# The last five groups of a gather-and-sum pass: what goes ahead of a group's sums, and in which order the sums go

## Chip, core and metric

The kernel runs on one core of a Trainium2 chip. The metric is the device time of one execution in microseconds. Five engines work beside each other and meet through semaphores: PE (TensorE, matrix products), DVE (VectorE), ACT (ScalarE), POOL (GpSimd) and SP (SyncE). DMAs are issued from SP, ACT and POOL. Each engine carries out its instructions in the order in which the program lists them.

## The reference, cut

One layer of a graph network over 12,500 nodes with 256 features and 200,000 edges (float32 throughout). The edges are sorted by destination.

```python
h = jnp.maximum(_layernorm(x, axis=-1), 0.0)
agg = jax.ops.segment_sum(h[src], dst, num_segments=N)
z = (1.0 + eps_gin) * h + agg
t = jnp.dot(z, W1) + b1                      # 256 -> 512
t = jax.nn.relu(_batchnorm(t, g1, bt1))      # over all nodes
conv_out = jnp.dot(t, W2) + b2               # 512 -> 256
out = jax.nn.relu(_batchnorm(conv_out + h, g2, bt2))
return x + out
```

The two batch norms need the mean and variance over all nodes, so the second product can't start before the first is complete for every node, and the output not before the second is.

## The kernel before

Three passes follow each other. The first makes t for all nodes and its statistics, the second makes conv_out + h and its statistics, the third the output. The change lies in the first.

Nodes are cut into NCH = 25 chunks of 512 (the last, chunk 24, has 212), edges into 1563 tiles of 128. GT = 12 tiles are a group, so there are NG = 131 groups, numbered 0 to 130; the last has three tiles. Since the edges are sorted, group i reaches nodes in a window of 256 from 96 i - 64 on; a program part not shown here takes over if they don't. For the end of the pass this gives: chunk 22 is last reached by group 123, chunk 23 by groups up to 128, chunk 24 by groups 127 to 130.

What is done for a group i, with the name of the helper:

- gather(i), L435: one indirect DMA on POOL per tile fetches 128 rows of h. The tiles of a group are fetched from the last to the first, each into its own slot of the group's buffer (gt, or gta and gtb together). There are five buffers, and gathers run AHEAD = 4 groups ahead.
- edges(i), L464: DVE builds the 0/1 matrices oh that say which edge goes to which of 128 node offsets.
- sums(i), L478: PE adds up, in one PSUM tile ps, twelve products of a slot's oh and its rows. The loop over j goes from slot 0 up, and slot 0 is the one fetched last.
- hold(i), L485: ACT copies ps to zs. spots(i), L489: DVE builds a matrix at that says where the 128 offsets lie in the window. put(i), L496: two products place zs in the window (pz).
- add(i), L507: DVE adds pz to the one or two chunks (zc) that the window reaches. z_load and z_scale fetch a chunk of transposed h and multiply it by 1 + eps.

Once the last group of a chunk has been added, its four slices follow: slice_of(c, f), L514, two products with W1 into ph (two PSUM buffers); take(c, f), L525 to L528, statistics on DVE, a copy to ts on ACT and a store of ts to t_tab issued by ACT.

All of the first pass is scheduled by hand: the loop at L550 writes the instructions out, and every engine keeps that order. A step i of this loop does, in this order: gather(i + 4), the adds up to group i - 4, take of the slice of the step before, spots and hold of group i - 2, edges(i + 1), sums(i), put(i - 2), and one slice from the queue of ready chunks. After the last group four more steps (131 to 134) bring the late groups in, with adds up to i - 3 and all queued slices.

Two lines that set this order:

```python
                    while added <= min(i - late, NG - 1):   # late: 4 for i < NG, else 3
                        add(added)
...
                    while whole < NCH and last(whole) < (before if i < NG else added):
                        queue += [(whole, f) for f in range(HC)]
```

After the loop, norm (L272 to L284) turns the statistics into scale and offset. The second pass (L623 on) loads a chunk of t (ti, three buffers, the first three loaded well before) and of transposed h (yT) on SP's queue, applies the activation on ACT (L630) and runs eight products per chunk into py (L637).

Of the kernel before, what the change touches and what calls it, by code (L numbers as in the profile page):

```python
# [19 lines left out]
AHEAD = 4  # L20
LEAD = 30
# [6 lines left out]
COPIES = 2  # L28
GROUP = 4
GAHEAD = 3  # L30


@with_exitstack
def kernel(
# [21 lines left out]
    HC = H // P  # L56
    CH = P * R
    NCH = -(-N // CH)
# [3 lines left out]
    for g in range(NCH):  # L62
        rows = min(CH, N - g * CH)
# [7 lines left out]
    full_tiles = E // P  # L71
    left = E - full_tiles * P
    NG = -(-NTILE // GT)
    STEP = -(-N * P * GT // E)
    WIDE = P + 2 * MARGIN
    NBLK = -(-max(NTILE, NG * GT) // P)
# [43 lines left out]
    def slot(ga, t):  # L120

        if len(ga) == 1:
            return ga[0][:, t, :]
        return ga[0][:, t, :] if t < LOW else ga[1][:, t - LOW, :]
# [26 lines left out]
    with ExitStack() as es:  # L151
# [5 lines left out]
        whole = E // PART  # L157
# [9 lines left out]
        with tc.issue_after(placed.ins):  # L167
# [30 lines left out]
        first = raw.tile([P, P], F32, name="first")  # L198
# [4 lines left out]
            pb, lhsT=first, rhs=dstT[:, : NG * GT].rearrange("p (g t) -> p g t", t=GT)[:, :, 0],  # L203
            start=True, stop=True,
# [42 lines left out]
        some = raw.tile([1, 1], F32, name="some")  # L247
# [59 lines left out]
    def fast():  # L307

        parts = []
        for n0, w in chunks:  # L310
            n = w * R
# [20 lines left out]
        with ExitStack() as fs:  # L332
# [8 lines left out]
            with ExitStack() as es:  # L341
# [87 lines left out]
                def gather(i):  # L429
                    t0, n = groups[i]  # L430
                    k = i % (AHEAD + 1)
                    ga = lands[k] if k < EARLY else (gat.tile([P, GT, D], F32, name="gt"),)
                    for t in reversed(range(t0, t0 + n)):
                        rows = left if t == full_tiles else P
                        nc.gpsimd.indirect_dma_start(  # L435
                            out=slot(ga, t - t0)[:rows], out_offset=None, in_=x if i < LEAD else h_tab,
                            in_offset=bass.IndirectOffsetOnAxis(ap=srcT[:rows, t : t + 1], axis=0),
                        )
                    gathered[i] = ga
# [16 lines left out]
                def z_scale(c):  # L456
                    n = chunks[c][1] * R
                    nc.scalar.activation(zc[c][:, :, :n], zc[c][:, :, :n], AF.Copy, scale=gin1)

                def edges(i):  # L460

                    t0, n = groups[i]
                    ohs[i] = sel.tile([P, GT, P], F32, name="oh", bufs=3)
                    nc.vector.tensor_tensor(  # L464
                        ohs[i][:, :n, :],
                        col[:, :P].unsqueeze(1).to_broadcast([P, n, P]),
                        dstT[:, t0 : t0 + n].unsqueeze(2).to_broadcast([P, n, P]),
                        op=OP.is_equal,
                    )

                def sums(i):

                    t0, n = groups[i]
                    ga, oh = gathered.pop(i), ohs.pop(i)
                    ps = ps_s.tile([P, D], F32, name="ps")
                    for j in range(n):
                        rows = left if t0 + j == full_tiles else P
                        nc.tensor.matmul(  # L478
                            ps, lhsT=oh[:rows, j, :], rhs=slot(ga, j)[:rows], start=(j == 0), stop=(j == n - 1)
                        )  # L480
                    summed[i] = ps

                def hold(i):
                    zss[i] = sel.tile([P, D], F32, name="zs", bufs=3)
                    nc.scalar.copy(zss[i], summed.pop(i))  # L485

                def spots(i):
                    ats[i] = sel.tile([P, WIDE], F32, name="at", bufs=3)
                    nc.vector.tensor_scalar(ats[i], col, shift[:, i : i + 1], None, op0=OP.is_equal)  # L489

                def put(i):

                    zs, at = zss.pop(i), ats.pop(i)
                    pz = ps_z.tile([P, DC, WIDE], F32, name="pz2")
                    for d in range(DC):
                        nc.tensor.matmul(  # L496
                            pz[:, d, :], lhsT=zs[:, d * P : (d + 1) * P], rhs=at, start=True, stop=True
                        )
                    placed[i] = pz

                def add(i):
                    lo, hi = span(i)
                    pz = placed.pop(i)
                    for c in reach(i):
                        a, b = max(lo, c * CH, 0), min(hi, (c + 1) * CH, N)
                        side = zc[c][:, :, a - c * CH : b - c * CH]
                        nc.vector.tensor_add(side, pz[:, :, a - lo : b - lo], side)  # L507

                def slice_of(c, f):

                    n = chunks[c][1] * R
                    ph = ps_t.tile([P, CH], F32, name="ph")
                    for d in range(DC):
                        nc.tensor.matmul(  # L514
                            ph[:, :n], lhsT=w1s[:, d, f * P : (f + 1) * P],
                            rhs=zc[c][:, d, :n], start=(d == 0), stop=(d == DC - 1),
                        )
                    slices[c, f] = ph
                    if f == HC - 1:
                        del zc[c]  # L520

                def take(c, f):
                    n = chunks[c][1] * R
                    ph = slices.pop((c, f))
                    nc.vector.bn_stats(st1[:, f, c, :], ph[:, :n])  # L525
                    ts = tsp.tile([P, CH], F32, name="ts")
                    nc.scalar.copy(ts[:, :n], ph[:, :n])  # L527
                    nc.scalar.dma_start(t_tab[c, :, f, :n], ts[:, :n])  # L528

                def first(c):  # L530

                    return min(i for i in range(NG) if c in reach(i))

                def last(c):
                    return max(i for i in range(NG) if c in reach(i))
# [6 lines left out]
                settle(gathered[0], GT // 2, GT, gathered[0], "g")  # L542
                queue, loads, scales, taken = [], {}, {}, []
                for c in range(NCH):
                    k = max(first(c) + 1, c + 2)
                    loads.setdefault(k, []).append(c)
                    scales.setdefault(max(first(c) + 3, c + 3), []).append(c)
                    assert c + 1 < k <= first(c) + 4 and c < LEAD - AHEAD
                added = whole = 0
                for i in range(NG + 4):  # L550
                    before = added
                    if i + AHEAD < NG:
                        gather(i + AHEAD)

                    late = 4 if i < NG else 3
                    while added <= min(i - late, NG - 1):
                        add(added)
                        added += 1
                    for c, f in taken:
                        take(c, f)  # L560
                    taken = []
                    if 0 <= i - 2 < NG:
                        spots(i - 2)
                        hold(i - 2)
                    if i + 1 < NG:
                        edges(i + 1)

                    if i < NCH:
                        h_chunk(i)
                    if i + 1 < min(LEAD, NG):  # L570
                        settle(gathered[i + 1], GT // 2, GT, gathered[i + 1], "g")
                    for c in scales.get(i, ()):
                        z_scale(c)

                    if i < NG:
                        sums(i)
                    if 0 < i <= NCH:
                        turn(i - 1)
                        turn_out(i - 1)
                    if 0 <= i - 2 < NG:  # L580
                        put(i - 2)
                    for c in loads.get(i, ()):
                        z_load(c)
                    while whole < NCH and last(whole) < (before if i < NG else added):
                        queue += [(whole, f) for f in range(HC)]
                        whole += 1
                    if i < NG:
                        some = queue[:1]
                    else:
                        some = queue  # L590
                    queue = queue[len(some):]
                    if i < NG:
                        for c, f in some:
                            slice_of(c, f)
                        taken = some
                    else:
                        for c, f in some:
                            slice_of(c, f)
                            take(c, f)
                assert added == NG and whole == NCH and not queue and not taken and not zc, (queue, taken, list(zc))  # L600

            sc1, of1 = norm(keep, st1, mv1, HC, g1c, bt1c, b1c, "1")

# [320 lines left out]
```

## Time and profile before

| | |
|---|---|
| Time, three runs | 2235.57 us median (2233.42 to 2241.05) |
| Profiled execution | 2235.88 us, span 2233.7 us |
| Granted PE clock over the span | 0.834 |
| PE busy, POOL busy | 1478.6 us, 1480.4 us |
| From the last gather to the first py | POOL's last gather starts at 1958.31, the first py at 2000.51 |
| Second pass on PE | 2000.51 to 2170.2 |
| End | 2233.7 |

How to read the rows: times are microseconds from the start of the span. A timeline row has start, duration, engine, line, operation, output and inputs, shapes and a count, and in brackets the idle time ahead of it with what ended it. Line numbers are those of the kernel before. A float32 matrix product leaves two records, so that twelve sums stand as x24. The ends of matmuls are modelled. A row of the chain has start, duration and what the time went to.

### The profile page before, as it was taken

To read this page: it belongs to the slowest core of one execution; us is meant where nothing else is said; L and a number is where in the kernel's file an instruction comes from. 1 tells how busy PE (TensorE), PEld (TensorE's weight loads), DVE (VectorE), ACT (ScalarE), POOL (GpSimd) and SP (SyncE) were. 2 spreads that over 40 slices of the span, in tenths; PEclk is the share of its full clock that TensorE was granted. 3 is DMA by queue.
4 is the path that set the end of the run, shared out by engine and by line. 5 is a ranking of instruction groups with operands and counts; after the bars stand their busy time and mean duration, and the time that the engine had idled before them with its cause. 6 is when DMAs were issued, how large, how long until landed. Compare 5 with 4: busy or idle time off the path is not lost.

```text
span 2233.7 us, 15142 instructions
## 1 busy us (share of the span) xinstructions
PE 1478.6 (66%) x4874; PEld 1066.5 (48%) x4874; DVE 716.5 (32%) x1092; ACT 510.1 (23%) x963; POOL 1480.4 (66%) x1575
## 2 busy tenths in 40 slices
PE   3567677667666666656666666666666666679994
PEld 2455545545444544544454444444444544444443
DVE  5566656531222122122212221211221121124345
ACT  4666666520000000000000000000000000034445
POOL 7777777777777777777777777777777777700000
PEclk9888888888888788878877887888887788789998
DMA  6677767644444444444444444444443444438739
GB/s 196 208 228 232 246 218 237 183 128 120 129 128 129 116 128 129 120 123 129 131 116 125 132 120 125 129 117 126 129 133 113 126 128 118 130 131 320 252 118 311
DMA packets 157615, 349.47 MB, mean 156 GB/s; under 512 B 30104, under 2 KB 82452, under 8 KB 154454
## 3 DMA queue, kind: packets, MB, share of 16 engines
q0 software_dynamic: 75008, 204.90, 32.8%
q1 hardware_dynamic: 54224, 104.03, 13.9%
q10 hardware_dynamic: 28294, 39.47, 4.9%
q8 instruction: 41, 0.67, 0.1%
q14 instruction: 48, 0.39, 0.1%
HBM read 284.28 MB, written 64.00 MB: 156 GB/s over the span
## 4 chain that ended last, share of the span: by engine, by line
POOL 52%; issue 22%; PE 11%; ACT 6%; DVE 4%; DMA 4%; ACTq 0%; SPq 0%; DVEq 0%; POOLq 0%
POOL gt L435 32%; POOL gta L435 12%; PE py L637 8%; POOL gtb L435 6%; DMA gt<-in_x_dram,srcT 3%; ACT gt L381 2%; DVE stg L370 2%; PE ps L478 2%; PE ph L514 1%; ACT yT L657 1%; ACT gta L381 1%; DMA out_dram<-xr 1%; DVE oh L464 1%; POOL gta L212 1%; ACT gtb L381 0%
## 5 line engine op out<-in xcount | busy, mean ns | idle before, releaser
L478 PE MATMUL ps<-gt,oh 128*128 128x256 f32 x1872 | 577.0, 481 | 402.5 <-DMA gt<-h_tab,srcT 321.5
L435 POOL DMA_INDIRECT gt<-h_tab,srcT x720 | 680.7, 945 | 219.3 <-issue 219.3
L478 PEld LDWEIGHTS ps<-gt,oh 128*128 128x128 f32 x1872 | 459.1, 250 | 546.0 <-issue 315.7
L478 PE MATMUL ps<-gta,oh 128*128 128x256 f32 x838 | 291.9, 524 | 270.5 <-DMA gta<-h_tab,srcT 212.1
L478 PEld LDWEIGHTS ps<-gta,oh 128*128 128x128 f32 x838 | 224.8, 275 | 352.4 <-issue 198.3
L525 DVE BATCH_NORM_STATS2 st<-ph 128x6 f32<-128x512 f32 (+1 forms) x100 | 68.4, 684 | 971.2 <-PE ph L514 971.2
L435 POOL DMA_INDIRECT gta<-h_tab,srcT x323 | 305.2, 945 | 98.4 <-issue 95.9
L527 ACT COPY ts<-ph 128x512 f32<-128x512 f32 (+1 forms) x100 | 57.4, 574 | 1326.5 <-DVE st L525 1326.5
L435 POOL DMA_INDIRECT gt<-in_x_dram,srcT x216 | 204.2, 945 | 65.8 <-issue 60.9
L464 DVE TENSOR_TENSOR oh<-col,dstT 128x1536 f32<-128x1536 f32 x131 | 227.7, 1738 | 0.0
L514 PE MATMUL ph<-zc,w1s 128*128 128x512 f32 (+1 forms) x400 | 193.1, 610 | 20.6 <-DVE hc L423 20.1
L507 DVE TENSOR_TENSOR zc<-pz,zc 128x512 f32<-128x512 f32 (+8 forms) x187 | 93.9, 520 | 282.5 <-PE pz L496 244.2
L435 POOL DMA_INDIRECT gtb<-h_tab,srcT x160 | 151.2, 945 | 48.7 <-issue 47.5
L637 PE MATMUL py<-gta,w2s 128*128 128x512 f32 (+1 forms) x400 | 169.6, 587 | 3.7 <-ACT gta L630 3.7
L496 PE MATMUL pz<-at,zs 128*128 128x256 f32 x524 | 134.9, 380 | 5.0 <-ACT zs L485 5.0
L637 PEld LDWEIGHTS py<-gta,w2s 128*128 128x128 f32 x400 | 76.4, 192 | 96.4 <-issue 75.7
L514 PEld LDWEIGHTS ph<-zc,w1s 128*128 128x128 f32 x400 | 78.3, 199 | 79.8 <-issue 49.1
L381 ACT ACTIVATE gt<-gt,nbg,rsg 128x256 f32<-128x256 f32 x216 | 108.1, 586 | 9.1 <-DVE nbg L379 8.1
L496 PEld LDWEIGHTS pz<-at,zs 128*128 128x128 f32 x524 | 97.6, 190 | 19.1 <-ACT zs L485 7.1
L630 ACT ACTIVATE gta<-ti,of,sc 128x512 f32<-128x512 f32 (+1 forms) x100 | 79.6, 803 | 82.9 <-PE py L637 78.8
L478 PE MATMUL ps<-gtb,oh 128*128 128x256 f32 x416 | 98.3, 379 | 0.0
L435 POOL DMA_INDIRECT gta<-in_x_dram,srcT x80 | 75.6, 946 | 24.4 <-issue 8.5
(97 smaller groups left out, 897.3 us busy)
## 6 DMA issues: line engine op xcount, KB each, us to landing
t_tab<-ts ACTq DMA_DIRECT2D x96, 256.0 KB
ti<-t_tab SPq DMA_DIRECT2D x24, 1024.0 KB
xt<-in_x_dram SPq DMA_DIRECT2D x24, 512.0 KB
h_tab<-ht ACTq DMA_DIRECT2D x24, 512.0 KB
h_cols<-hc SPq DMA_DIRECT2D x24, 512.0 KB
zc<-h_cols SPq DMA_DIRECT2D x24, 512.0 KB
yT<-h_cols SPq DMA_DIRECT2D x24, 512.0 KB
gt<-h_tab,srcT POOLq DMA_INDIRECT x720, 2.8
```

The lines of the kernel that those rows point to most:

```text
L370: nc.vector.bn_stats(st[:, c : c + 2, :].rearrange("p c s -> p (c s)"), two.rearrange("p c d -> p d c"),)
L381: nc.scalar.activation(slot(to, c), slot(v, c), AF.Relu, bias=nb[:, c : c + 1], scale=rs[:, c : c + 1])
L435: nc.gpsimd.indirect_dma_start(out=slot(ga, t - t0)[:rows], out_offset=None, in_=x if i < LEAD else h_tab, in_offset=bass.IndirectOffsetOn ...
L464: nc.vector.tensor_tensor(ohs[i][:, :n, :], col[:, :P].unsqueeze(1).to_broadcast([P, n, P]), dstT[:, t0 : t0 + n].unsqueeze(2).to_broadcas ...
L478: nc.tensor.matmul(ps, lhsT=oh[:rows, j, :], rhs=slot(ga, j)[:rows], start=(j == 0), stop=(j == n - 1))
L496: nc.tensor.matmul(pz[:, d, :], lhsT=zs[:, d * P : (d + 1) * P], rhs=at, start=True, stop=True)
L507: nc.vector.tensor_add(side, pz[:, :, a - lo : b - lo], side)
L514: nc.tensor.matmul(ph[:, :n], lhsT=w1s[:, d, f * P : (f + 1) * P], rhs=zc[c][:, d, :n], start=(d == 0), stop=(d == DC - 1),)
L525: nc.vector.bn_stats(st1[:, f, c, :], ph[:, :n])
L527: nc.scalar.copy(ts[:, :n], ph[:, :n])
L630: nc.scalar.activation(tT[:, f, :n], ti[:, f, :n], AF.Relu, bias=of1[:, f : f + 1], scale=sc1[:, f : f + 1],)
L637: nc.tensor.matmul(py[:, :n], lhsT=w2s[:, f, d * P : (d + 1) * P], rhs=tT[:, f, :n], start=(f == 0), stop=(f == HC - 1),)
```

## The change

A constant CLOSE = 5 cuts the loop in two. Steps 0 to 125 run as before (without the cases that only the end needed). Steps 126 to 131 have a loop of their own:

- spots(i), spots of the two groups still open, edges(i + 1) and the scaling of chunk 24 come first; chunk 24 is loaded in step 125 and scaled in step 126 (before: 128 and 130).
- Then every earlier group is finished ahead of this group's sums: hold and put of each group up to i - 1, and all adds up to i - 1.
- Then all slices of chunks that are complete by now, each with its take.
- Then sums(i), with the slots in the order in which they were fetched, from the last slot down to slot 0.

In the listing of the changed program's instructions this gives, on PE: placing of 124 and 125, four slices of chunk 22, sums of 126; placing of 126, sums of 127; placing of 127, sums of 128; placing of 128, four slices of chunk 23, sums of 129; placing of 129, sums of 130; placing of 130, four slices of chunk 24. POOL's and SP's lists are the same as before; of SP's waits, the loads of the first yT no longer stand behind late stores of ts: the first waits for a load of its own queue, the second and third for the second and third store of chunk 23.

```diff
+CLOSE = 5
...
                     ps = ps_s.tile([P, D], F32, name="ps")
-                    for j in range(n):
+                    order = list(range(n)) if i < NG - CLOSE else list(reversed(range(n)))
+                    for j in order:
                         rows = left if t0 + j == full_tiles else P
                         nc.tensor.matmul(
-                            ps, lhsT=oh[:rows, j, :], rhs=slot(ga, j)[:rows], start=(j == 0), stop=(j == n - 1)
+                            ps, lhsT=oh[:rows, j, :], rhs=slot(ga, j)[:rows], start=(j == order[0]), stop=(j == order[-1])
                         )
...
                 for c in range(NCH):
-                    k = max(first(c) + 1, c + 2)
+                    k = min(max(first(c) + 1, c + 2), NG - CLOSE - 1)
                     loads.setdefault(k, []).append(c)
-                    scales.setdefault(max(first(c) + 3, c + 3), []).append(c)
+                    scales.setdefault(min(max(first(c) + 3, c + 3), NG - CLOSE), []).append(c)
...
-                for i in range(NG + 4):
+                for i in range(NG - CLOSE):
...
+                near = NG - CLOSE - 2
+                for c, f in taken:
+                    take(c, f)
+                for i in range(near, NG - CLOSE):
+                    spots(i)
+                for i in range(NG - CLOSE, NG + 1):
+                    if i + AHEAD < NG:
+                        gather(i + AHEAD)
+                    if i < NG:
+                        spots(i)
+                    if i + 1 < NG:
+                        edges(i + 1)
+                    for c in scales.get(i, ()):
+                        z_scale(c)
+                    while near < i:
+                        hold(near)
+                        while added < near - 1:
+                            add(added)
+                            added += 1
+                        put(near)
+                        near += 1
+                    while added < near:
+                        add(added)
+                        added += 1
+                    while whole < NCH and last(whole) < added:
+                        queue += [(whole, f) for f in range(HC)]
+                        whole += 1
+                    for c, f in queue:
+                        slice_of(c, f)
+                        take(c, f)
+                    queue = []
                     if i < NG:
-                        for c, f in some:
...
+                        sums(i)
```

More of the change, by code (lines that the diff above doesn't have):

```diff
@@ L73 @@
     NG = -(-NTILE // GT)
+    assert max(LEAD, NCH) < NG - CLOSE
     STEP = -(-N * P * GT // E)
@@ L544, in fast @@
                 for c in range(NCH):
-                    k = max(first(c) + 1, c + 2)
+                    k = min(max(first(c) + 1, c + 2), NG - CLOSE - 1)
                     loads.setdefault(k, []).append(c)
-                    scales.setdefault(max(first(c) + 3, c + 3), []).append(c)
+                    scales.setdefault(min(max(first(c) + 3, c + 3), NG - CLOSE), []).append(c)
                     assert c + 1 < k <= first(c) + 4 and c < LEAD - AHEAD
                 added = whole = 0
-                for i in range(NG + 4):
+                for i in range(NG - CLOSE):
                     before = added
[L552 to L556, printed above, removed]
+                    gather(i + AHEAD)
+                    while added <= i - 4:
                         add(added)
@@ L560, in fast @@
                         take(c, f)
-                    taken = []
-                    if 0 <= i - 2 < NG:
+                    if i >= 2:
                         spots(i - 2)
                         hold(i - 2)
-                    if i + 1 < NG:
-                        edges(i + 1)
+                    edges(i + 1)
                     if i < NCH:
                         h_chunk(i)
-                    if i + 1 < min(LEAD, NG):
+                    if i + 1 < LEAD:
                         settle(gathered[i + 1], GT // 2, GT, gathered[i + 1], "g")
@@ L573, in fast @@
                         z_scale(c)
-                    if i < NG:
-                        sums(i)
+                    sums(i)
                     if 0 < i <= NCH:
@@ L579, in fast @@
                         turn_out(i - 1)
-                    if 0 <= i - 2 < NG:
+                    if i >= 2:
                         put(i - 2)
@@ L583, in fast @@
                         z_load(c)
-                    while whole < NCH and last(whole) < (before if i < NG else added):
+                    while last(whole) < before:
                         queue += [(whole, f) for f in range(HC)]
                         whole += 1
-                    if i < NG:
[L588 to L591, printed above, removed]
-                    if i < NG:
-                        for c, f in some:
[L594 to L599, printed above, removed]
@@ L600, in fast @@
-                assert added == NG and whole == NCH and not queue and not taken and not zc, (queue, taken, list(zc))
+                    taken = queue[:1]
+                    queue = queue[1:]
+                    for c, f in taken:
+                        slice_of(c, f)
+                near = NG - CLOSE - 2
+                for c, f in taken:
+                    take(c, f)
[3 more added lines that the diff above has]
+                    if i + AHEAD < NG:
+                        gather(i + AHEAD)
+                    if i < NG:
+                        spots(i)
+                    if i + 1 < NG:
+                        edges(i + 1)
+                    for c in scales.get(i, ()):
[14 more added lines that the diff above has]
+                    for c, f in queue:
+                        slice_of(c, f)
+                        take(c, f)
+                    queue = []
+                    if i < NG:
+                        sums(i)
@@ L602, in fast @@
+                assert added == near == NG and whole == NCH and not zc, list(zc)
             sc1, of1 = norm(keep, st1, mv1, HC, g1c, bt1c, b1c, "1")
```

## The prediction

> **What bounds the kernel now.** I read the page's busy times first, then the chain that ended last, then the timelines of the engines around the end of the gathers.
>
> ```profile
> PE 1478.6 (66%) x4874; PEld 1066.5 (48%) x4874; DVE 716.5 (32%) x1092; ACT 510.1 (23%) x963; POOL 1480.4 (66%) x1575
> POOL 52%; issue 22%; PE 11%; ACT 6%; DVE 4%; DMA 4%; ACTq 0%; SPq 0%; DVEq 0%; POOLq 0%
> ```
>
> PE and POOL have the same share of the span, but the chain goes through POOL and its issue gaps for 74%: the gathers set the pace. On POOL's timeline one gather starts every 1.25 us (0.95 busy, 0.30 between) without a break, up to these:
>
> ```profile
> 1954.59 0.94 POOL L435 DMA_INDIRECT gt<-h_tab,srcT  x1 [0.30 <-issue]
> ...
> 1958.31 0.95 POOL L435 DMA_INDIRECT gta<-h_tab,srcT  x1 [0.30 <-issue]
> ```
>
> These are the last gathers of groups 129 and 130 (130 has three). After them nothing is left for POOL, and the chain of waits runs over PE:
>
> ```profile
> 1954.59 4.04 DMA gt<-h_tab,srcT
> 1958.77 8.08 PE ps L478 x24
> 1967.71 1.73 PE ph L514 x4
> ...
> 1990.22 1.15 PE pz L496 x4
> 1991.78 3.21 PE ph L514 x8
> 2000.51 169.65 PE py L637 x400
> ```
>
> From the landing of group 129 at 1958.77 to the first product of the second pass (py) at 2000.51 lie 41.7 us. This is the only place where the change can bring something, and the change lies in it. PE's timeline shows what fills it (24 records are 12 matmuls, two records each):
>
> ```profile
> 1942.44 7.72 PE L478 MATMUL ps<-gt,oh 128*128 128x256 f32 x24 [5.73 <-DMA gt<-h_tab,srcT]
> 1950.86 1.88 PE L514 MATMUL ph<-zc,w1s 128*128 128x512 f32 x4
> 1958.77 8.08 PE L478 MATMUL ps<-gt,oh 128*128 128x256 f32 x24 [6.03 <-DMA gt<-h_tab,srcT]
> ...
> 1969.27 1.65 PE L478 MATMUL ps<-gta,oh 128*128 128x256 f32 x6
> 1971.61 1.13 PE L496 MATMUL pz<-at,zs 128*128 128x256 f32 x4 [0.69 <-ACT zs L485]
> 1972.58 1.88 PE L514 MATMUL ph<-zc,w1s 128*128 128x512 f32 x4
> 1976.63 1.13 PE L496 MATMUL pz<-at,zs 128*128 128x256 f32 x4 [2.18 <-ACT zs L485]
> 1977.60 10.44 PE L514 MATMUL ph<-zc,w1s 128*128 128x512 f32 x20
> 1990.22 1.13 PE L496 MATMUL pz<-at,zs 128*128 128x256 f32 x4 [2.18 <-ACT zs L485]
> 1991.78 5.02 PE L514 MATMUL ph<-zc,w1s 128*128 128x212 f32 x16 [0.42 <-DVE zc L507]
> 2000.51 9.69 PE L637 MATMUL py<-gta,w2s 128*128 128x512 f32 x18 [3.71 <-ACT gta L630]
> ```
>
> PE idles some 6 us ahead of each group, since the sums begin with the slot that lands last; then 12 sums run in one burst, 8 us behind the landing. Behind it wait placings that are two groups late and seven wide slices (one at 1967.71, one at 1972.58, five from 1977.60) that could have run earlier: chunk 22 has its last edges in group 123 and chunk 23 in group 128.
>
> **The change part by part.**
>
> *Sums in the order of landing.* No instruction is added. At full clock a sum takes 0.43 us, from the row below with 16 records of double width in 6.80 us (0.425 us each, two to a matmul, half the width), at half clock twice that. One group arrives in 12 x 1.25 = 15 us, so PE keeps up, and only the last sum is left when the last slot lands.
>
> ```profile
> 1974.40:1977.80 3.40, 1.22 (x6) 1.00 0.20 77
> 1977.80:1981.20 3.40, 3.40 (x5) 0.50 0.00 0
> 1981.20:1988.00 6.80, 6.80 (x16) 1.00 0.51 162
> 1988.10:1991.50 3.40, 1.13 (x4) 1.00 0.70 234
> 1991.50:1994.90 3.40, 3.12 (x9) 0.50 0.84 280
> 2005.10:2170.00 164.90, 164.90 (x394) 1.00 0.68 243
> ```
>
> The columns are window, length, PE busy, granted clock, DMA share, GB/s. Windows with PE busy for a third (1.22 and 1.13 of 3.40) are each followed by one at half clock, and busy stretches return to full. A trickle of one sum in 1.25 us is a third busy at full clock (0.43) and two thirds at half (0.85), so I expect it to swing between both and cost the last sums nothing but 0.4 us each. The Trainium skill, TensorE: Matmul & The Clock Gate, "HAM oscillation — how this bites in real kernels", speaks against such spreading: it has work gathered into dense stretches so that the array is not put back to half clock. The two rows agree that thin windows are punished; what a punished trickle would make of the time is the first rival.
>
> *Placing, adds and ready slices ahead of the sums.* At step 126 PE now places groups 124 and 125 and runs the four slices of chunk 22 before group 126; this delays the sums of 126 by at most 4 x 3.4 us at half clock, which 127 and 128 make up, each having 15 us for 5.1 to 10.2 us of sums. The buffers cost nothing: the only gather still to be issued then, group 130, waits for the sums of 125, as before. At step 129 PE places group 128 and runs the four slices of chunk 23, under the landing of 129. The end then goes so, with these rows for copies, adds and landings:
>
> ```profile
> 1971.18 0.37 ACT L485 COPY zs<-ps 128x256 f32<-128x256 f32 x1 [0.40 <-PE ps L478]
> 1970.47 0.48 DVE L507 TENSOR_TENSOR zc<-pz,zc 128x320 f32<-128x320 f32 x1
> 1972.13 0.36 DVE L507 TENSOR_TENSOR zc<-pz,zc 128x192 f32<-128x192 f32 x1 [1.18 <-ACT zc L458]
> 1991.39 0.33 DVE L507 TENSOR_TENSOR zc<-pz,zc 128x168 f32<-128x168 f32 x1 [1.79 <-PE pz L496]
> gt<-h_tab,srcT POOLq DMA_INDIRECT x24, 2.7
> gta<-h_tab,srcT POOLq DMA_INDIRECT x3, 3.3
> gt<-h_tab,srcT POOLq DMA_INDIRECT x2, 4.0
> t_tab<-ts ACTq DMA_DIRECT2D x1, 256.0 KB
> ```
>
> Three rows of gathers end with the median from issue to landing: in a quiet stretch (1925 to 1954), for the three gathers of 130, and for two gathers beside the store in the last row (both from 1954 to 1963).
>
> 1. Group 128 lands at 1942.4; its last sum ends at 1943.3 (before 1942.44 + 7.72 = 1950.2). Copy 0.4, placing 1.0, two adds 0.8: chunk 23 is ready at 1945.6.
> 2. Four slices of 1.72 us, of which I let a window at half clock stretch one by 1.7: 8.6 us, to 1954.2. (All full 1952.5, all half 1959.3.)
> 3. Sums of 129, most of which have landed: 5.1 us, to 1959.3. The landing allows no earlier end: 1954.59 + 4.0 + one sum is 1959.2.
> 4. Copy and placing of 129: 1.5, to 1960.8; its add runs on DVE beside what follows.
> 5. Group 130: the last gather is issued at 1958.31. Quiet it lands at 1961.0, by its own row at 1961.6. Now four 256 KB stores of chunk 23 and two 512 KB loads of yT (which wait in their queue for two of these stores, and so start far earlier than before) fall in the same 10 us; one such store cost 1.3 us. I take 4.3 us: 1962.6, and bounds of 2.7 and 6.0 (2.7 and two and a half times the 1.3). Its last sum ends at 1963.4.
> 6. Copy 0.45, placing 1.13, add 0.4: the four narrow slices of chunk 24 start at 1965.4, where before they start at 1991.78.
> 7. From there to the first py it took 2000.51 - 1991.78 = 8.73 us (slices, statistics, norm, first activation). Nothing in it is changed: py starts at 1974.1.
>
> That is 26.4 us earlier. What follows (169.65 us of py, then the third pass) moves as one piece: PE is busy 164.90 of 164.90 us there, and its inputs are requested by the same activations. The profiled execution took 2235.88 us with a span of 2233.7; the median of the three runs is 2235.57, so both give the same base. 2235.88 - 26.4 = 2209.5.
>
> *The early load and scaling of chunk 24* lie at steps 125 and 126, with POOL's 15 us steps as cover: ACT is in no step of the chain there. Zero; without cover the scaling of 424 columns would be 0.6 us, by the 0.37 us for 256. *DVE's order*: the four statistics of chunk 23 follow their slices at a slice's pace. Zero.
>
> **The rivals.**
>
> *PE falls behind at half clock (2221.8).* For it: thin windows are followed by half clock. If everything from 1945.6 ran at half: slices to 1959.3, sums of 129 to 1969.5, placing 2.1, sums of 130 2.6, then 2.5 to the narrow slices at 1976.7, and 9.7 instead of 8.7 to py: 1986.4, so 14.1 us gained, 2221.8 at the worst point. Against: a dense stretch of 6.80 us at 1981.20 was at full clock right after one at half, and slices and sums of 129 form such a stretch.
>
> *The gain doesn't come through (about 2233).* The second pass might be held by its loads, so that an earlier start is given back as PE waits. For it: 243 GB/s over the pass. Against: py waited 3.71 us once, for an activation, and the chain shows one piece of 400 records. I put what would be left at the run-to-run spread, some 3 us.
>
> *Each sum that waits alone costs more than a gather (2254, slower).* The mechanism: a sum queued on its own landing can't have its weights loaded in advance.
>
> ```profile
> L478 PE MATMUL ps<-gt,oh 128*128 128x256 f32 x1872 | 577.0, 481 | 402.5 <-DMA gt<-h_tab,srcT 321.5
> L478 PEld LDWEIGHTS ps<-gt,oh 128*128 128x128 f32 x1872 | 459.1, 250 | 546.0 <-issue 315.7
> ```
>
> Unoverlapped, two records of 0.481 and two loads of 0.250 are 1.46 us, above the 1.25 us of a gather. Then PE, which comes to the bulk of group 126 at about 1914 (three groups of 15 us ahead of 1958.77), needs for four groups 4 x (17.5 + 2.6), for chunk 23 9, for group 130 4.4, then 2.0 and 8.7: py at 2018.5, 18 us later than now. The point from which it is slower: 51 sums share 2000.5 - 1914 - 10.4 - 9 - 10.7 = 56.4 us, 1.1 us each. Against: a PE that is behind doesn't wait any more, and then runs at the pace of the burst, 8.08 us for 12.
>
> **How the numbers follow.** About 0.3% (6.7 us) is what a measurement of this kernel can tell from no change. Forecast as worked out: 0.82. PE behind at half clock: 0.08; it is still faster by over 0.3%. Gain given back: 0.05, within 0.3%. Sums slower than gathers: 0.05, slower. So faster 0.90, same 0.05, slower 0.05. The forecast's own bounds: last landing after 2.7 us instead of 4.3 and narrow slices at full clock (the first took 1.8 instead of 0.7) give 2.7 less, and the runs spread by some 2 below their median: 2205. Upward, landing 1.7 later, placings at half clock 0.7 each, and two more half-clock windows at the second pass's start at 1.7 each make 6.5, 2216; three more take in the better part of the first rival: 2219.
>
> **What would show it.** In the changed profile: the sums of 128 and 129 as single records spread over the gathers, without idle stretches of 6 us; wide slices at about 1945 to 1954 and none after 1960; from the last POOL gather to the first py some 15 us instead of 41; py again about 170 us. I am wrong if sums of 129 end later than 1963, if the last gather takes over 6 us to land, or if py's stretch grows.

## The result

The changed kernel takes 2214.74 us (median of four runs, 2213.96 to 2218.58) against 2235.53 us before; the ratio is 0.991, with a 95% interval of 0.9893 to 0.9927. It is faster by 20.8 us; the forecast, 2209.5 us with a range of 2205 to 2219, is 26.0 below that base. In a second comparison, beside later kernels, it took 2215.2 us (ratio 0.9908, 0.9891 to 0.9924).

A measure that helps below is the **stretch**: from the start of the last gather to the first py. It was 1958.31 to 2000.51, 42.2 us, before. The forecast's sum makes it 15.8 us (1974.1 - 1958.31). Each stretch below is that of one profiled execution. PE's timeline of the changed kernel, from the sums of group 128 on (start, duration, line, what, count, idle before):

```profile
1943.18 5.34 PE L481 MATMUL ps<-gt,oh 128*128 128x256 f32 x24
1948.99 1.13 PE L499 MATMUL pz<-at,zs 128*128 128x256 f32 x4 [0.46 <-ACT zs L488]
1950.51 7.13 PE L517 MATMUL ph<-zc,w1s 128*128 128x512 f32 x16 [0.38 <-DVE zc L510]
1957.48 4.05 PE L481 MATMUL ps<-gt,oh 128*128 128x256 f32 x18
1963.27 0.70 PE L481 MATMUL ps<-gt,oh 128*128 128x256 f32 x2 [1.74 <-DMA gt<-h_tab,srcT]
1965.16 2.08 PE L481 MATMUL ps<-gt,oh 128*128 128x256 f32 x4 [1.20 <-DMA gt<-h_tab,srcT]
1967.70 2.07 PE L499 MATMUL pz<-at,zs 128*128 128x256 f32 x4 [0.46 <-ACT zs L488]
1969.70 3.22 PE L481 MATMUL ps<-gta,oh 64*128 64x256 f32 x6
1973.39 1.75 PE L499 MATMUL pz<-at,zs 128*128 128x256 f32 x4 [0.46 <-ACT zs L488]
1975.56 3.92 PE L517 MATMUL ph<-zc,w1s 128*128 128x212 f32 x16 [0.43 <-DVE zc L510]
1983.18 27.27 PE L659 MATMUL py<-gta,w2s 128*128 128x512 f32 x57 [3.70 <-ACT gta L652]
```

The last gather of this execution starts on POOL at

```profile
1963.81 0.95 POOL L437 DMA_INDIRECT gta<-h_tab,srcT  x1 [0.30 <-issue]
```

so the stretch is 1983.18 - 1963.81 = 19.4 us (19.8 in the second profiled execution of the same kernel, from the second comparison). It saves 22.8 us. Before, all twelve sums of 129, seven wide slices and three late placings stood behind the landing of 129, beside the sums and the placing of 130; now only its last three sums (PE waits for their rows) and its placing do, beside those of 130, and no wide slice.

The last gather starts 5.5 us later than in the execution of before. That can't be put down to the change: in the second execution of the changed kernel it starts at 1959.34, and in the other kernels with the same gathers between 1958.3 and 1964.0. A gather takes 947 ns in the mean here and took 945 there, and POOL is busy for 4.8 us longer in all. The stretch is free of it, and the medians are over runs in which it varies.

The forecast's stretch is missed by 3.6 us. The windows around the end show where (window, length, PE busy, granted clock, DMA share, GB/s; PE alone, from the second execution, whose last gather starts at 1959.34):

```profile
1953.10:1957.20 4.10, 4.04 (x19) 1.00 0.73 172
1957.20:1960.80 3.60, 0.70 (x2) 0.98 0.92 362
1960.80:1965.40 4.60, 4.05 (x8) 0.50 0.43 144
1965.40:1971.10 5.70, 5.24 (x11) 0.52 0.00 0
1971.50:1975.50 4.00, 3.67 (x16) 1.00 0.13 42
```

PE stands idle while the DMA engines move 362 GB/s, and then works 10 us at half clock. The transfers of the first execution from 1957 to 1972 are:

```profile
yT<-h_cols SPq DMA_DIRECT2D x2, 512.0 KB
t_tab<-ts ACTq DMA_DIRECT2D x2, 256.0 KB
gt<-h_tab,srcT POOLq DMA_INDIRECT x4, 5.8
gta<-h_tab,srcT POOLq DMA_INDIRECT x3, 5.2
```

A gather lands after 5.2 to 5.8 us, twice the quiet 2.7. The loads of yT are there because the stores that they wait for in SP's queue come earlier (SP still waits for stores of ts twice, 22.2 us in all, where it waited three times, 69.3 us, before). SP's rows for the first three, in the changed kernel and in the kernel before (start of the first, time from there to the end of the last):

```profile
1937.97 23.25 SPq L649 DMA_DIRECT2D yT<-h_cols  x3
```

```profile
1984.64 5.99 SPq L627 DMA_DIRECT2D yT<-h_cols  x3
```

The first is issued 26 us before the last gather, while PE is still behind with earlier sums; the issue of the last of the three ends at 1961.2, just as the last gathers are issued.

### The profile page after: what moved, and what is told of

Its sections match the earlier page's. It is cut to its first block, busy times and chain, and to the rows that moved or that the text cites. A ratio compares the mean times of both kernels' runs of the same rounds, so it can differ in the third digit from the quotient of the medians.

```text
span 2216.6 us, 15137 instructions
## 1 busy us (share of the span) xinstructions
PE 1472.6 (66%) x4874; PEld 1060.2 (48%) x4874; DVE 716.4 (32%) x1092; ACT 509.8 (23%) x963; POOL 1485.2 (67%) x1575
## 4 chain that ended last, share of the span: by engine, by line
POOL 52%; issue 22%; PE 10%; DMA 6%; ACT 6%; DVE 4%; ACTq 0%; DVEq 0%; POOLq 0%
POOL gt L437 33%; POOL gta L437 12%; PE py L659 8%; POOL gtb L437 6%; DMA gt<-in_x_dram,srcT 3%; ACT gt L383 2%; PE ps L481 2%; ACT yT L679 1%; DVE stg L372 1%; DMA gta<-in_x_dram,srcT 1%; PE ph L517 1%; ACT gta L383 1%; POOL gta L214 1%; DVE oh L466 1%; PE pz L499 0%
## 5 line engine op out<-in xcount | busy, mean ns | idle before, releaser
L481 PE MATMUL ps<-gt,oh 128*128 128x256 f32 x1872 | 561.8, 471 | 367.9 <-DMA gt<-h_tab,srcT 284.7
L481 PEld LDWEIGHTS ps<-gt,oh 128*128 128x128 f32 x1872 | 447.1, 243 | 505.8 <-issue 249.7
L481 PE MATMUL ps<-gta,oh 128*128 128x256 f32 x838 | 302.9, 539 | 296.3 <-DMA gta<-h_tab,srcT 231.7
L481 PEld LDWEIGHTS ps<-gta,oh 128*128 128x128 f32 x838 | 232.3, 285 | 380.9 <-issue 238.4
L517 PE MATMUL ph<-zc,w1s 128*128 128x512 f32 (+1 forms) x400 | 187.6, 595 | 17.5 <-DVE hc L425 16.5
```

The lines of the kernel that those rows point to most:

```text
L481: nc.tensor.matmul(ps, lhsT=oh[:rows, j, :], rhs=slot(ga, j)[:rows], start=(j == order[0]), stop=(j == order[-1]))
L517: nc.tensor.matmul(ph[:, :n], lhsT=w1s[:, d, f * P : (f + 1) * P], rhs=zc[c][:, d, :n], start=(d == 0), stop=(d == DC - 1),)
```

## The experiments

All ratios are against the kernel before on the same chip. "Late yT" and the like are names of this text.

**Order alone.** The kernel before, with only the loop in sums turned round:

```diff
-                    for j in range(n):
+                    order = list(range(n)) if i < NG - CLOSE else list(reversed(range(n)))
+                    for j in order:
...
```

> The kernel before, with only the order of the sums reversed in the last five groups. Measure beside the time: the stretch from the start of the last gather to the first py, 42.2 us before and 19.4 us with the whole change. My theory: the two parts act on different work, and the order alone takes away the burst of 129 behind its landing, 8.1 us less one last sum: stretch about 35, time about 2228.5. Rival (the late placings and slices hide it, since PE has seven wide slices to run anyway): stretch 40 to 42, time 2234.

Measured: 2227.57 us, ratio 0.9966 (0.9954 to 0.9979). PE's timeline, last gather at 1958.33:

```profile
1951.43 0.70 PE L480 MATMUL ps<-gt,oh 128*128 128x256 f32 x2 [0.85 <-DMA gt<-h_tab,srcT]
1953.84 4.31 PE L480 MATMUL ps<-gt,oh 128*128 128x256 f32 x10 [1.71 <-DMA gt<-h_tab,srcT]
1957.98 1.03 PE L498 MATMUL pz<-at,zs 128*128 128x256 f32 x4
...
1968.90 8.75 PE L516 MATMUL ph<-zc,w1s 128*128 128x512 f32 x20
1990.06 10.12 PE L639 MATMUL py<-gta,w2s 128*128 128x512 f32 x19 [3.71 <-ACT gta L632]
```

The sums of 129 are finished at 1958, some 8.7 us earlier than before, and the stretch is 1990.06 - 1958.33 = 31.7 us, 3.3 less than I expected: 1.5 since the sums end earlier than my 8.1 less one last sum, and 1.7 since the five queued slices now run at full clock (8.75 us instead of 10.44). Alone, the order is worth 10.5 us of this execution's stretch and 8 us in the medians (the interval goes from 5 to 10); that it would be hidden is out. Here PE takes many of the sums one by one as they land, and it keeps up. The clock swings as the prediction expected; PE's windows of this run (window, length, PE busy, granted clock, DMA share, GB/s), the first with mostly single sums, the second right behind it:

```profile
1929.00:1937.00 8.00, 5.62 (x18) 0.93 0.36 108
1937.50:1943.00 5.50, 5.32 (x10) 0.50 0.40 117
```

**Schedule alone.** The changed kernel with `order = list(range(n))` in all groups.

> The changed kernel, with the sums in the old order (slot 0 first) in all groups. My theory: the burst of 129 comes back behind the landing, ten sums more than the two that remain now, at half clock since PE idles for the landing: 6 to 8 us, stretch 26, time 2221. Rival (the order brings nothing once the slices are out of the way): stretch 19 to 20, time 2214.5.

Measured: 2211.95 us, ratio 0.9897 (0.988 to 0.9913). My expectation fell. The last gather starts at 1960.63, and the stretch is 19.4 us, exactly that of the whole change:

```profile
1944.76 8.23 PE L481 MATMUL ps<-gt,oh 128*128 128x256 f32 x24 [4.89 <-DMA gt<-h_tab,srcT]
1953.45 1.13 PE L499 MATMUL pz<-at,zs 128*128 128x256 f32 x4 [0.46 <-ACT zs L488]
1954.96 7.13 PE L517 MATMUL ph<-zc,w1s 128*128 128x512 f32 x16 [0.38 <-DVE zc L510]
1961.93 5.34 PE L481 MATMUL ps<-gt,oh 128*128 128x256 f32 x24
...
1980.00 20.42 PE L659 MATMUL py<-gta,w2s 128*128 128x512 f32 x43 [3.71 <-ACT gta L652]
```

From the sums of 128 to the narrow slices PE has no pause but some 0.4 to 0.5 us each for a copy or an add. The burst of 128 comes behind its landing, so the slices of chunk 23 end only at 1961.9; by then group 129 has landed, its twelve sums go in 5.34 us at full clock, and nothing waits for a gather. So two different chains give the same 19.4 us: with the old order PE's own work, with the order of landing something that PE waits for. No run shows a reason for the equal lengths. What PE waits for is the question of the next run.

**Late yT.** The changed kernel; a 0.19 us copy on ACT behind the copy of group 130's sums marks the end, and one of the first yT tiles can't be loaded before it:

```diff
...
                         hold(near)
+                        if near == NG - 1:
+                            nc.scalar.copy(mark, zss[near][:, :1])
...
+                    if k == 0:
+                        nc.gpsimd.tensor_copy(yT[g][:, 0, :1], marks[0])
                     nc.sync.dma_start(yT[g], h_cols[g, :, :, :n])
```

> The changed kernel; one of the first three yT loads and with it the queue behind it waits until the sums of group 130 have been copied, so that two 512 KB loads are out of the way of the last gathers (one stays early, where it is in the changed kernel too). My theory of the 3.6 us by which the stretch is longer than forecast: these loads and the four stores share the DMA engines with the last gathers. Then the median from issue to landing of the last three gathers falls from 5.2 us to 3.5 to 4 us, and the stretch from 19.4 to about 17; time 2212. Rival a (the stores alone do it): landing stays at 5 and stretch at 19. Rival b (the half clock of the placings, not the landing, is what is missing): landing falls, stretch stays within 0.7 of 19.4.

Measured: 2208.87 us, ratio 0.9883 (0.9866 to 0.9899). Last gather at 1964.04; landings from 1957 to 1972, and PE's timeline:

```profile
gt<-h_tab,srcT POOLq DMA_INDIRECT x4, 4.3
gta<-h_tab,srcT POOLq DMA_INDIRECT x3, 2.9
```

```profile
1957.83 4.05 PE L484 MATMUL ps<-gt,oh 128*128 128x256 f32 x18
1962.45 1.50 PE L484 MATMUL ps<-gt,oh 128*128 128x256 f32 x4 [0.57 <-DMA gt<-h_tab,srcT]
1964.47 0.70 PE L484 MATMUL ps<-gt,oh 128*128 128x256 f32 x2 [0.52 <-DMA gt<-h_tab,srcT]
1965.63 1.13 PE L502 MATMUL pz<-at,zs 128*128 128x256 f32 x4 [0.46 <-ACT zs L491]
1966.69 1.76 PE L484 MATMUL ps<-gta,oh 64*128 64x256 f32 x6
...
1978.09 22.38 PE L666 MATMUL py<-gta,w2s 128*128 128x512 f32 x46 [3.70 <-ACT gta L659]
```

The stretch falls from 19.4 to 14.05 us, by 5.3 and not the 2.4 I expected, because the half clock goes with the late landing. The longest wait of PE for a gather shrinks from 1.74 to 0.57 us, and the last sum of 129 ends 1.1 us after the last gather's start instead of 3.4: 2.3 us. The placing of 129 takes 1.13 instead of 2.07 us, the sums of 130 1.76 instead of 3.22, and from that last sum to the narrow slices it is 5.3 us instead of 8.3: 3.0 us. So the two loads of yT, which are needed only by the second pass, cost the changed kernel 5.3 us of stretch. Both rivals are out as the main cause. In time the interval just overlaps with that of the changed kernel; the landings and the stretch are what shows it.

**Slices behind the sums.** The changed kernel, with the loop over the queue behind sums(i):

```diff
+                    if i < NG:
+                        sums(i)
                     for c, f in queue:
                         slice_of(c, f)
                         take(c, f)
                     queue = []
-                    if i < NG:
-                        sums(i)
```

> The changed kernel, with the ready slices of a step run behind its sums and not ahead. The four slices of chunk 23 then stand between the sums of 129 and the placing of 129, and stores and yT loads come later. My theory: the gathers then land in 2.7 to 3.3 us, 129 is done some 3 us after the last gather's start at the latest, and 6.9 us of slices follow where the changed kernel lost some 4 us to late landing and half clock: stretch 20 to 22, time 2216. Rival (slices ahead are worth all of their PE time): stretch 26, time 2221.

Measured: 2217.12 us, ratio 0.9921 (0.9904 to 0.9937). Last gather at 1959.00:

```profile
1954.56 4.78 PE L481 MATMUL ps<-gt,oh 128*128 128x256 f32 x8 [0.30 <-DMA gt<-h_tab,srcT]
1959.13 8.56 PE L517 MATMUL ph<-zc,w1s 128*128 128x512 f32 x16
1969.87 1.13 PE L499 MATMUL pz<-at,zs 128*128 128x256 f32 x4 [2.18 <-ACT zs L488]
...
1982.33 17.84 PE L659 MATMUL py<-gta,w2s 128*128 128x512 f32 x37 [3.70 <-ACT gta L652]
```

The stretch is 23.3 us, above my 20 to 22 and below the rival's 26. The gathers land in 2.7 us, as expected, but the last sums of 129, single ones again, and the slices behind them ran into half clock (4.78 us for four sums, 8.56 for four slices), and the copy of 129 stands behind the last take in ACT's queue (2.18 us of waiting). Of the 8.56 + 2.18 us that stand in the way here, the changed kernel saves only some 3.5 to 4: the rest it loses again to late landings and the half clock that they bring. With late yT, which keeps the slices ahead, 9.3 us are saved.

**Late yT, stores late too.** As late yT, with eight ts buffers, and the four stores of chunk 23 issued only behind the mark:

```diff
+                    if c == NCH - 2:
+                        held.append((c, f, n, ts))
+                    else:
+                        nc.scalar.dma_start(t_tab[c, :, f, :n], ts[:, :n])
...
+                            for c, f, n, ts in held:
+                                nc.scalar.dma_start(t_tab[c, :, f, :n], ts[:, :n])
```

> The kernel with yT late, and the four stores of chunk 23 issued only after the sums of group 130 have been copied (eight ts buffers instead of four). My theory (of the late landing most is due to the yT loads, the rest to these stores): the three gathers of 130 land in 2.7 to 2.9 us, those before in 2.8 instead of 4.3, and the stretch goes from 14.1 to 13 to 13.5 us, since only the last landing sets the end: time 2207.5 to 2208.5. Rival (stores matter as much as loads): stretch 11 to 12, time 2206.

Measured: 2207.26 us, ratio 0.9872 (0.9856 to 0.9889), the fastest of all. Last gather at 1961.15; landings from 1953 to 1970, and PE's timeline:

```profile
gt<-h_tab,srcT POOLq DMA_INDIRECT x5, 2.8
gta<-h_tab,srcT POOLq DMA_INDIRECT x3, 2.6
```

```profile
1954.83 4.91 PE L484 MATMUL ps<-gt,oh 128*128 128x256 f32 x22
...
1974.34 26.05 PE L673 MATMUL py<-gta,w2s 128*128 128x512 f32 x54 [3.71 <-ACT gta L666]
```

All gathers land at the quiet pace, and the stretch is 13.2 us, as expected. So of the late landing's 6.2 us (19.4 to 13.2) the loads make 5.3 and the stores 0.9. In time the intervals of this kernel and of late yT overlap. The 0.9 rests on one execution of each, and two of the changed kernel lie 0.4 apart; that the landing falls from 4.3 to 2.8 us agrees with it.

**Old order, late yT**, to see whether the order of landing is worth something once nothing collides:

> The changed kernel with yT late and the sums in the old order (slot 0 first). If the order of landing is worth nothing by itself, this equals the kernel with yT late in the order of landing (stretch 14.1, time 2208.9). My theory: the order was worth its 5 us all along and only the yT loads ate it; with the old order the slices of chunk 23 end some 7 us later, the yT loads come after the last gathers anyway, and keeping them late changes nothing: stretch 18 to 19.5, time 2211 to 2212.

Measured: 2213.13 us, ratio 0.99 (0.9884 to 0.9917); the last gather starts at 1958.36 and

```profile
1959.69 5.34 PE L484 MATMUL ps<-gt,oh 128*128 128x256 f32 x24
...
1977.76 22.56 PE L666 MATMUL py<-gta,w2s 128*128 128x512 f32 x48 [3.71 <-ACT gta L659]
```

The stretch is 19.4 us, as with early yT and the old order: the loads cost nothing where PE's own work is the chain. (The time is 1 us above what I expected.) With late yT the order is worth 19.4 - 14.05 = 5.3 us of stretch; with the loads where the change puts them, nothing.

**The change again**, beside the last two:

> The changed kernel itself, beside the next two on one chip. With the whole change 2214.7 us, with the schedule alone 2211.95: was that a difference of the runs, or does the order of landing cost something? My theory (with the order, sums and slices run some 7 us earlier against the gathers, and so bring stores and yT loads into the landing of the last gathers): 2214 to 2215, above the schedule alone by about 2. Rival (order worth nothing either way): 2212.

2215.2 us, at the upper end of what I expected. But the stretch, 19.8, is only 0.4 above the schedule's alone, not 2. Some 2 to 3 us between these medians are thus not in the stretch; their intervals overlap (0.9891 to 0.9924 and 0.988 to 0.9913). From the first py to the end it is 234.7 us here and 232.8 in both kernels with the old order, 1.9 us more, of which py makes 1 (170.60 us in the chain instead of 169.65). Why the pass takes longer here stays open.

## Why the prediction was right, and where its sizes were off

*The place and the mechanism* were right: the whole gain lies between the last gather and the first py, the burst and the wide slices left it, and what follows moved almost as a piece (py 170.49 us instead of 169.65; from the first py to the end 233.4 us, and 234.7 in the second execution, instead of 233.2). But the forecast took both parts of the change for gains, and one of them paid nothing here: with the old order the changed kernel has the same stretch of 19.4 us. The placings and slices ahead of the sums brought the gain alone, and the order of landing only pays once the yT loads are out of its way. The time lies within the range because its upper part left room for a later landing and for placings at half clock. The schedule alone (2211.95 us) would have come out in it as well, so that the number says nothing for the order of landing: so far it was luck.

*Steps 1 and 2* hold. The sums of 128 end 15.3 us ahead of the last gather's start (forecast 15.0). The slices of chunk 23 take 7.13 us, all at full clock, where I had given 8.6. The sign I had named, single records spread over the gathers, appears with the order alone; in the changed kernel the work of step 126 (two placings, chunk 22's four slices, and a wait of 4.38 us for DVE's add ahead of them) puts PE behind, and in this execution groups 126 to 128 go in dense bursts of 5.34 us until PE has caught up.

*Step 3 is the one that failed*, though the time lies in the range. I took 4.0 us for the last landing of 129, from a row with one store beside it, and let only group 130 feel the yT loads. They reach 129 as well: nine sums are done in 4.05 us, and then PE waits 1.74 and 1.20 us for gathers that land after 5.8 us in the median. The last sum ends 3.4 us after the last gather's start; forecast 1.0.

*Steps 4 to 6* were mis-sized through the clock. The wait of step 3 made a thin window, and the 10 us behind it ran at about half clock (0.50 and 0.52 in the second execution): placing 2.07 and 1.75 instead of 1.0 and 1.13, sums of 130 3.22 us behind the placing. I had listed this as an upper bound of 0.7 for each placing. The landing of 130 itself (5.2 us, forecast 4.3) is covered by it. The sums of 130 end at 9.1 us of the stretch instead of 5.1. *Step 7* gave 1.1 us back: 7.62 us, since the narrow slices now run at full clock.

*The rivals.* PE fell behind at half clock only in these 10 us, not from the slices on. But for 0.2 to 1.5 us the gain wasn't lost behind the first py. Sums waiting alone don't cost more than a gather: the rival's premise holds (the weights of the sum at 1963.27 are loaded from 1963.26 on, when its rows have landed), but with the order alone the sums follow the gathers, a sum by itself takes 0.70 us at full clock and not the rival's 1.46, and the last sum of 129 ends at 1958.0, ahead of the start of the last gather. The page of the Trainium skill on the clock gate that I weighed (TensorE: Matmul & The Clock Gate, "HAM oscillation — how this bites in real kernels") is borne out in part. Its rule is against PE idle gaps of more than some 3.4 us; here two waits of 1.74 and 1.20 us with one sum between them were enough to bring half clock back. But what paid was removing the gap's cause, not gathering the sums: with late yT the old order, which runs them in one burst, has a stretch that is 5.3 us longer.

## What to carry to other kernels

Work pulled ahead of a wait brings its transfers with it, and also lets everything that was queued on them start earlier; look up which queue these release, and what is still landing then. When a part of a change shows no effect, ask which chain sets the end without it: here two chains of equal length hid that the order of landing is worth 5.3 us once the loads are late. Measure the stretch that the change touches, from an event that it can't move, rather than the whole time, where another engine's pace varies by more.

## What the runs showed of the hardware

Two 512 KB loads and some 256 KB stores beside the gathers doubled a gather's time to landing, from 2.7 us to between 5.2 and 5.8 us; in the same place of the second execution the DMA engines moved 362 GB/s. With the loads held back, the gathers beside the stores landed after 4.3 us. A PE window of 3.6 us with 0.70 us of work was followed by 10 us at half clock, though PE was busy for 9.3 of these 10.3 us. I had expected that a busy stretch would be granted full clock sooner: in the kernel before, a window of 3.4 us at 0.50, busy throughout, was followed by one at 1.00. Why it took longer here stays open.
